# The last inverse transform of a convolution layer: transposes first, products by halves, output sent by halves

## The chip, the cores and the metric

The kernel runs on one core of a Trainium2 chip. The metric is the device time of one execution in microseconds. A time "of the profile" is on the clock of the one execution that was profiled, counted from its first instruction.

## The reference

The program has two layers on an image `x` of 2 x 128 channels x 64 x 64, that is 4096 tokens of 128 channels for each of two batches. Layer 0 is a group norm, a projection to queries, keys and values with rotary positions, attention with four heads, and a residual. Layer 1 is attention of the normalised tokens with themselves, and then a spectral unit: a causal convolution of the tokens with 16 filters, taken through Fourier transforms, mixed by matrices, plus a sum over three shifted copies of the tokens. Cut to what matters here:

```python
def _stu_conv(phi, u, n):
    Vf = jnp.fft.rfft(phi, n=n, axis=0)
    Uf_p = jnp.fft.rfft(u, n=n, axis=1)
    ...
    U_plus = jnp.fft.irfft(Vf[None, :, :, None] * Uf_p[:, :, None, :], n=n, axis=1)[:, :sl]
...
def _stu(u, sigma, phi, Mu, Mpp, Mpm):
    return _compute_spectral(u, sigma, phi, Mpp, Mpm) + _compute_ar_u(Mu, u)
...
t = t + _L1_attn_ref(_ln_t(t))
t = t + _L1_ffn_ref(_ln_t(t), ...)
x = _from_tokens(t, x)
```

`_compute_spectral` mixes the convolved signals with 2 x 16 matrices of 128 x 128. The result has the shape of `x`.

## The kernel before

Layer 0 runs first, then the attention of layer 1, then the spectral unit. The spectral unit writes a position as 32 j + i with j from 0 to 127 and i from 0 to 31, transforms along j with products on TensorE against a table of cosines and sines, convolves along i with the filters at each frequency, mixes with the matrices, and transforms back along j.

The last stage of the program goes through four passes, (batch, parity) = (0, 0), (0, 1), (1, 0), (1, 1), where the parity `ro` is that of i. In each pass there are eight chunks `ch` of frequencies and two signs `s`. For each, `chunk` loads filter tables (through SyncE's queue) and transformed tokens (through GpSimd's), `convolve` makes products `cv` and splits them into a high part `xh` (copied by ScalarE) and a low part `xl` (a subtraction on VectorE), and `mix` (L1208) multiplies both parts by the matrices and sums into `acc`, which at the end of a chunk is copied to a quarter of `oh`, 512 columns at a time (L1219). `mix` of a step is laid between the pieces of `convolve` of the next step, so TensorE always has products that wait for nothing. Tiles of `xh` come from a pool with two buffers of one tag; a new tile of the tag takes the place of the one before the last and waits for its readers.

`back` is the inverse transform of one pass. It takes the 16 blocks of i of its parity in four groups `p4` of four. For each group `turned` starts a load of `had` (256 KB: what the residual and the shifted copies add to the output) on SyncE's queue (L1238), transposes four 128 x 128 tiles for each of two parts c, cosine and sine (L1249), and copies them out of PSUM, part 0 on VectorE and part 1 on ScalarE, into `v` (L1250). `inverse` then makes eight products `bk` (L1258), two for each block, with a tile of `v` as the stationary operand and the 128 columns of `gw[:, c, :]` as the moving one, and adds `had` on VectorE into the output tile (L1260). That add writes every 32nd column, as the output is in the order of positions.

In three of the four passes `back` is a generator whose pieces are laid between those of the next pass. In the last pass (`end`) there is nothing to lie between. There the order is written out by hand: `turned(0)`, then for each group `turned` of the next one and `inverse` of this one; `v` takes buffers of the tag `xh`; the two parts of the transposes go to the two banks of one PSUM tile `pair` of the tag `cv`, which has three buffers; `had` is one buffer. At the very end the output of the batch goes to memory in four transfers of 512 KB, two from SyncE's queue and two from ScalarE's (L1275).

`ordered` keeps TensorE's instructions in the order of the program text. The waits between engines are worked out by the framework from which tile each instruction reads and writes. After the network, every engine reads a flag and branches over a second, general version of the network, which these inputs do not need.

## Time and profile before

| what | value |
|---|---|
| median of 3 runs | 2941.99 us (2936.91, 2941.99, 2942.27) |
| the profiled execution, its own time | 2936.34 us |
| span of the profile, first to last instruction | 2934.5 us |
| TensorE matmul busy | 2855.1 us, 97% of the span |
| VectorE / ScalarE / GpSimd busy | 58% / 65% / 23% |
| mean granted clock of TensorE | 0.992 |
| last mixing product to last instruction | 2903.9 to 2934.5 us |

PE stands for TensorE's products and PEld for its loads of the stationary operand, which overlap them; DVE is VectorE, ACT ScalarE, POOL GpSimd, SP SyncE, and a q behind a name means that engine's queue of instructions or transfers. A row of the timeline is: start in us, length in us, engine, line, operation, result <- operands, shapes, how many in a row, and in brackets the idle time before and what ended it. A row of the chain is: start, length, engine, what, how many. The output add stands in a row as `out<-bk,had`. A product in fp32 appears as two records. `first` and `m` are the PSUM tiles of layer 0's first projections and of the mixing.

### The profile page before, as it was taken

How to read it: one execution, taken by the hardware profiler on the slowest of the kernel's cores; microseconds unless marked ns; L12 is line 12 of the kernel's file. 1: busy time of each engine (PE TensorE's matmuls, PEld its weight loads, DVE VectorE, ACT ScalarE, POOL GpSimd, SP SyncE). 2: the span in 40 equal slices, each digit the busy share in tenths (PEclk: the TensorE clock that was granted, in tenths of full speed). 3: DMA queues.
4: the chain of work that ended last, by engine and by line, in shares of the span. 5: the costliest groups of instructions: out<-in, count | busy, mean ns of one | idle time of the engine just before them, and what ended most of it. 6: DMA issues, size and time to landing. Idle time of an engine off the chain costs nothing. (4 is left out here: it accounts for less than half of the span.)

```text
span 2934.5 us, 40078 instructions
## 1 busy us (share of the span) xinstructions
PE 2855.1 (97%) x13872; PEld 1817.6 (62%) x13872; DVE 1691.6 (58%) x2916; ACT 1916.2 (65%) x2507; POOL 660.9 (23%) x1328
## 2 busy tenths in 40 slices
PE   4999999999999999999999999999999999999997
PEld 2555555555455578787777885566666666666665
DVE  5264563255243289877766676555555555555553
ACT  4999999999999955565555664444444444444442
POOL 4031120022000010000102003434444444444440
PEclk9999999999999999999999999999999999999999
DMA  5021120021000024100011003333333334333331
GB/s 145 29 82 54 47 63 20 5 78 48 6 33 35 4 86 127 55 1 1 26 40 39 8 26 72 94 87 98 88 86 82 81 82 115 81 86 82 82 81 47
DMA packets 165777, 175.91 MB, mean 60 GB/s; under 512 B 45264, under 2 KB 109536, under 8 KB 165568
## 3 DMA queue, kind: packets, MB, share of 16 engines
q1 hardware_dynamic: 121760, 136.00, 16.7%
q0 software_dynamic: 40816, 34.04, 5.5%
q10 hardware_dynamic: 2992, 3.22, 0.3%
q8 instruction: 115, 1.88, 0.3%
q14 instruction: 94, 0.77, 0.1%
HBM read 130.68 MB, written 25.49 MB: 53 GB/s over the span
## 5 line engine op out<-in xcount | busy, mean ns | idle before, releaser
L433 ACT ACTIVATE e<-s 128x1536 f16<-128x1536 f32 (+1 forms) x704 | 936.7, 1428 | 35.8 <-PE s L190 30.9
L1186 DVE TENSOR_TENSOR xl<-cv,xh 128x1024 fp32r<-128x1024 f32 x512 | 603.3, 1220 | 436.6 <-ACT xh L1185 349.2
L1185 ACT CAST xh<-cv 128x1024 fp32r<-128x1024 f32 x512 | 494.6, 1018 | 523.1 <-PE cv L1176 511.7
L1151 POOL DMA_DIRECT2D tokens_in<-rows x1024 | 490.8, 487 | 680.6 <-PE cv L1176 577.7
L190 PE MATMUL s<-qs,ks 128*128 128x512 f16 x2048 | 557.4, 379 | 8.5 <-ACT e L433 3.4
L190 PE MATMUL acc<-e,v 128*97 128x512 f16 x2048 | 557.3, 379 | 3.4 <-DVE accs L389 0.2
L1208 PE MATMUL m<-xh,loT 128*128 128x512 f32 x1024 | 410.0, 400 | 0.0
L1208 PE MATMUL m<-xh,hiT 128*128 128x512 f32 x1024 | 403.5, 394 | 0.0
L190 PEld LDWEIGHTS <-v 128*97 128x97 bf16 x2048 | 254.6, 124 | 214.5 <-issue 12.3
L190 PEld LDWEIGHTS <-ks 128*128 128x128 f16 x2048 | 200.5, 99 | 227.6 <-issue 42.5
L910 ACT ACTIVATE ey<-y,nshift 128x512 f32<-128x512 f32 x288 | 195.9, 689 | 201.4 <-PE y L901 179.6
L1176 PE MATMUL cv<-tables_in,tokens_in 32*128 32x512 f32 x2048 | 299.4, 645 | 1.8 <-DVE xl L1186 1.8
L1208 PE MATMUL m<-xl,hiT 128*128 128x512 f32 x1024 | 292.3, 417 | 1.2 <-DVE xl L1186 0.5
L1208 PEld LDWEIGHTS m<-xl,hiT 128*128 128x128 f32 x1024 | 178.9, 189 | 175.8 <-issue 104.7
L1208 PEld LDWEIGHTS m<-xh,loT 128*128 128x128 f32 x1024 | 192.7, 188 | 90.8 <-issue 47.8
L1208 PEld LDWEIGHTS m<-xh,hiT 128*128 128x128 f32 x1024 | 192.6, 188 | 42.3
L920 DVE TENSOR_TENSOR eT<-eT,eT 128x512 fp32r<-128x512 f32 x224 | 147.5, 685 | 113.4 <-ACT eT L919 112.1
L927 PE MATMUL oacc<-ep,hi 128*128 128x512 f32 x576 | 210.4, 414 | 1.2 <-DVE ep L959 1.1
L389 DVE COPY accs<-acc 97x512 f32<-97x512 f32 x64 | 44.2, 691 | 275.2 <-PE acc L190 275.2
L959 DVE TENSOR_TENSOR ep<-ey,ep 128x512 fp32r<-128x512 f32 x288 | 191.5, 685 | 7.7 <-ACT ep L958 1.6
L919 ACT ACTIVATE eT<-eT 128x512 fp32r<-128x512 f32 x224 | 133.1, 605 | 55.6 <-PE eT L917 55.4
L927 PE MATMUL oacc<-eT,hi 128*128 128x512 f32 x448 | 154.1, 405 | 2.8 <-DVE oT L967 1.6
(192 smaller groups left out, 3045.2 us busy)
## 6 DMA issues: line engine op xcount, KB each, us to landing
tables_in<-tables SPq DMA_DIRECT2D x1024, 64.0 KB, 3.3
tab<-in_rot SPq DMA_DIRECT2D x32, 512.0 KB, 4.1
tokens_in<-rows POOLq DMA_DIRECT2D x1024, 16.0 KB, 3.2
qs<-term POOLq DMA_DIRECT2D x128, 64.0 KB, 2.2
rows<-uh SPq DMA_DIRECT2D x64, 128.0 KB, 1.9
ks<-term POOLq DMA_DIRECT2D x96, 64.0 KB, 1.9
accs<-back SPq DMA_DIRECT2D x32, 128.0 KB, 2.3
lows<-stage SPq DMA_DIRECT2D x16, 256.0 KB, 2.0
```

The costliest lines, as they stand in the source:

```text
L190: tc.keep_in_program_order(nc.tensor.matmul(*args, **kw))
L433: nc.scalar.activation(e[:, own, :], ps[:, own, :], AF.Exp, scale=SCORE_SCALE)
L910: nc.scalar.activation(e[:, 2 * h + q, :], ps[:, q, :], AF.Exp, bias=nshift, accum_out=den[:, t, i : i + 1])
L919: nc.scalar.activation(eT[0], pt, AF.Copy, accum_out=den[:, 4 * i + u, j : j + 1])
L920: nc.vector.tensor_tensor(eT[1], pt, eT[0], ALU.subtract)
L927: nc.tensor.matmul(acc, a[0][:, own], c, start=(start and t == 0 and n == 0), stop=(stop and t == len(es) - 1 and n == 2),)
L959: nc.vector.tensor_tensor(es[t][1], e[:, t, :], es[t][0], ALU.subtract)
L1151: nc.gpsimd.dma_start(ut[part, :, :], rows[b][ci, row : row + BP, w0 : w0 + WC // 2, :])
L1176: nc.tensor.matmul(pu[:, h, :], ut[grp, w % 2, :], tt[grp, w % 2, :], start=True, stop=True)
L1185: nc.scalar.copy(hi, pu.rearrange("d h (c k) -> d k h c", k=NK))
L1186: nc.vector.tensor_tensor(seconds[n % 2][:, :, w, 64 * g2 : 64 * g2 + 64].rearrange("d k (h c) -> d k h c", h=2), pu.rearrange("d h (c k) ...
L1208: nc.tensor.matmul(acc, m, x, start=(s == 0 and w == 0 and i == 0), stop=(s == 1 and w == WC - 1 and i == len(products) - 1),)
```

## The change

It touches only the last pass of `back`, the one with `end`. One tile `whole` of the tag `xh` holds all four groups: for each, four slots of 128 columns for `had` and eight for `v`. `turned` runs for all four groups first, so the four loads of `had`, the 32 transposes and the 8 copies come ahead of every product. Then the products go by halves `n` of the transformed length: for each half and each pair of groups a PSUM tile `pair` of two banks is taken, and each group's eight products write 4 x 64 columns into its bank, from the same stationary tiles and half the columns of `gw`. An add of half a group follows. After the four adds of a half, two of the four output transfers are started, one on SyncE's queue and one on ScalarE's.

```diff
-                had = p.tile([P, 4, P], F32, tag="had", name=f"had{u}", bufs=1)
+                if end:
+                    had, v = whole[:, p4, :4], whole[:, p4, 4:].rearrange("p (c q) x -> p c q x", c=2)
+                else:
+                    had = p.tile([P, 4, P], F32, tag="had", name=f"had{u}", bufs=1)
+                    v = p.tile([P, 2, 4, C], F32, tag="v", name=f"v{u}", bufs=1)
                 nc.sync.dma_start(had, baser[:, ro, 4 * p4 : 4 * p4 + 4, :])
-
-                v = (pf if end else p).tile(
-                    [P, 2, 4, C], F32, tag="xh" if end else "v", name=f"v{u}", bufs=2 if end else 1
-                )
...
-            ahead = list(turned(0)) if end else None
+            if end:
+                whole = pf.tile([P, BP // 4, 12, P], F32, tag="xh", name="whole", bufs=2)
+                parts = [list(turned(p4))[-1] for p4 in range(BP // 4)]
+                for n in range(2):
+                    js = bass.ts(n, P // 2)
+                    for p8 in range(BP // 8):
+                        pair = pc.tile([P, 2, 512], F32, tag="cv", name=f"bk{n}_{p8}", bufs=3)
+                        for h in range(2):
+                            p4 = 2 * p8 + h
+                            had, v = parts[p4]
+                            pt = pair[:, h, : 2 * P].rearrange("p (q j) -> p q j", q=4)
+                            for q in range(4):
+                                for c in range(2):
+                                    ordered(
+                                        nc.tensor.matmul(
+                                            pt[:, q, :], v[:, c, q, :], gw[:, c, js], start=(c == 0), stop=(c == 1)
+                                        )
+                                    )
+                            nc.vector.tensor_tensor(
+                                outr[:, ro, 4 * p4 : 4 * p4 + 4, js], pt, had[:, :, js], ALU.add
+                            )
+                    for i in range(2):
+                        cols = bass.ts(2 * n + i, L // 4)
+                        (nc.scalar if i % 2 else nc.sync).dma_start(io["out"][b][:, cols], outs[b][:, cols])
+                return
             for p4 in range(BP // 4):
-                if end:
-                    parts = ahead[-1]
-                    ahead = list(turned(p4 + 1)) if p4 + 1 < BP // 4 else None
-                else:
-                    for parts in turned(p4):
-                        yield
+                for parts in turned(p4):
+                    yield
                 inverse(p4, *parts)
                 yield
```

## The prediction

> **What bounds the kernel now.** I read the page first, then the chain of work that ended last, then the timeline of the last 35 us, which is all that the diff can touch: apart from renamed tiles, every engine's instruction order before the last block's transposes is the same in both programs.

> ```profile
> span 2934.5 us, 40078 instructions
> PE 2855.1 (97%) x13872; PEld 1817.6 (62%) x13872; DVE 1691.6 (58%) x2916; ACT 1916.2 (65%) x2507; POOL 660.9 (23%) x1328
> ```

> TensorE holds the kernel for 97% of the span, and the change leaves that alone. What it edits is the tail after TensorE's last mixing product, where no engine is full. The chain, in order of time (start, length, what):

> ```profile
> 2892.44 11.42 PE m L1208 x48
> ...
> 2903.89 0.59 ACT oh L1219
> ...
> 2906.02 1.17 PE vt L1249 x8
> 2907.19 0.02 issue
> 2907.22 0.70 DVE v L1250
> ...
> 2916.93 1.80 PE bk L1258 x16
> 2918.73 0.02 issue
> 2918.76 1.03 DVE out L1260
> 2919.79 0.02 issue
> 2919.81 2.92 DMA had<-base
> ...
> 2922.82 1.02 DVE out L1260
> ```

> The reader is to see a ladder: transposes, copy, products (1.80 each block), add, and in the last block a load of `had` that ends after the products. The timeline adds both ends of it:

> ```profile
> 2919.83 2.05 PE L1258 MATMUL bk<-gw,v 128*128 128x128 f32 x16 [1.12 <-DVE out L1260]
> 2922.82 1.02 DVE L1260 TENSOR_TENSOR out<-bk,had 128x512 f32<-128x512 f32 x1 [3.04 <-DMA had<-base]
> 2923.87 0.83 SPq L1275 DMA_DIRECT2D out<-out  x2
> ```

> The last products end at 2921.88, their add begins at 2922.82: 0.94 us for `had`. The four output transfers (2.1 MB) go out together at 2923.87; the stretches of 1 us after it move 123, 397, 389, 418, 373, 369, 61 GB/s, so the data flow from about 2924.7 to 2930.15 at some 390 GB/s. The span ends at 2934.5, 10.66 us after the last add.

> What the change turns on is the price of a product with 64 moving columns in place of 128. Layer 0 has products of just that form, and the timeline of weight loads shows both:

> ```profile
> 30.83 0.86 PEld L190 LDWEIGHTS first<-wv,xn 128*128 128x128 f32 x7 [0.24 <-issue]
> 2908.40 1.87 PEld L1258 LDWEIGHTS bk<-gw,v 128*128 128x128 f32 x16
> ```

> The first has 64 moving columns, the second 128. A load lasts 0.19, so the steps are (0.86 - 0.19) / 6 = 0.112 and (1.87 - 0.19) / 15 = 0.112 us. Half the columns, the same step: the weight load sets it.

> [...]

> **The change part by part.** Times are on the trace's clock; the oh copy ends at 2904.48 in both.

> *Transposes first.* Before, a block's second four transposes wait for the vector copy of the first four, because both write one tile of two banks; the changed program keeps that wait. The pace without products between is the one from 2906.02 to 2907.96: 1.94 us (1.16 of transposes, 0.70 copy, gaps). So second halves begin at 2906.02, 2907.96, 2909.90, 2911.84. Products follow 0.55 after a second half (2907.96 to 2908.51): first product 2912.39. The ScalarE copies (0.59 each) end within 1.5 us of their transposes, ahead of the products that need them.

> *Products by halves.* Eight groups of eight products, each two records: 16 x 0.112 = 1.80 us, as much as a whole block now. TensorE's work here goes from 4 x 1.80 = 7.2 to 14.4 us: +7.2. The stationary operand is the transposed block, so each is loaded twice.

> *A new wait.* Two groups share one tile of two banks. The changed program's order shows the second group waiting for the vector engine's count that the add of the first raises: the same rule that stalls the transposes. Behind that product stand all later ones, so it is paid four times. Each costs what a non-waiting group hides: products end, add, restart. From the trace: 1.99 us from a running group's start to its add (2908.51 to 2910.50), 2.08 when the group starts after a wait (2919.83 to 2921.88, plus 0.03), 0.05 from an add's end to the products.

> *The add of half a block*, 256 elements. Not in the trace. [...] Lower bound the contiguous 0.42, upper the whole block's 1.02. I take 0.59, since the excess over the contiguous add should go with elements.

> So: add 1 begins 2912.39 + 1.99 = 2914.38. A pair takes 0.59 + 0.05 + 2.08 to its second add, and 1.80 more to the next pair's first: 4.52. Add 4 ends at 2914.38 + 4.52 + 2.72 + 0.59 = 2922.21; add 8 at 2914.38 + 3 x 4.52 + 2.72 + 0.59 = 2931.25. Before it was 2923.84: +7.41.

> *Halves of the output.* The first two transfers go at about 2922.2 and by the rates above are in by about 2926.4; 5 us of products cover them. After add 8 only 1.05 MB are left in place of 2.1: 1.05 / 0.39 = 2.7 us less. The end: 2931.25 + 10.66 - 2.7 = 2939.2. If nothing were gained by sending early, +2.7. On SyncE and ScalarE only the second half's transfers stand behind the first's, and those are ready later anyway; ScalarE's copies are all ahead of them. GpSimd's queue issues nothing in this stretch.

> *Loads of `had`.* Now four into one tile, which takes the place of the `xh` of the step before the last, read by TensorE until 2891.92. SyncE is done with tables by then. Four issues of 0.38 and 3.0 to land put them in by 2897, under mixing products, 17 us before the first add. The 0.94 us wait goes (it is inside the sum); without that cover 1.05 MB at the 230 GB/s of the present loads would cost some 4.5 us.

> Sum: +7.4 - 2.7 = **+4.7 us on the span of 2934.5, so 2939.2**. The profiled execution took 2936.34; the median of three is 2941.99 (2936.91 to 2942.27), so the profile sits at the low end. I put the difference on the median: 2941.99 + 4.7 = **2946.7 us**, 0.16% slower, inside the 0.2% that a measurement of this kernel can tell from no change.

> **The rivals.**
> 1. *Half an add costs nearly a whole one* (the slower side). If the excess of L1260 sits in each instruction rather than each element, four exposed adds cost up to 1.02 for 0.59: +1.7, so +6.4, 2948.4, 0.22%. For it: a single size in the trace. Against it: the contiguous rows scale. It passes 0.2% (5.9 us) once the add takes 0.89.
> 2. *No wait within a pair.* Then eight groups run on at 1.80: the last add begins at 2912.39 + 7 x 1.80 + 1.99 = 2926.98, 3.7 earlier: +1.0, 2943.0. Against it: the transposes of this very tile stall so in the trace.
> 3. *Half the columns, half the time.* Groups of 0.9: each pair saves 1.8, 7.2 in all: -2.5, 2939.5. Against it: the row of layer 0.
> 4. *The change doesn't do what it says*: the first half's output is held until the second's goes. Then -2.7 is lost: +7.4, 2949.4. Against it: its wait names only the first four adds.

> **How the numbers follow.** My account 0.64, rival 1 0.12, rival 2 0.08, rival 3 0.05, rival 4 0.04, other 0.07. Faster by over 0.2% comes from almost none of them: rival 3 with a low median. But +4.7 stands only 1.2 us below the bound, and three runs spread over 5.4 us, so of my own account I give a third to slower; with two thirds of rival 1, rival 4 and half of the rest that makes slower 0.37, faster 0.05, same 0.58. The range: rivals 2 and 3 with a median at the low end reach 2940; rivals 1 and 4 with one at the high end reach 2951. My account's own is 2942 to 2949.

> **What would show it.** Eight groups of `bk` with 64 columns, weight loads of 1.87 us per 16; four waits of TensorE for the adds, 0.7 us each (0.03 + 0.59 + 0.05; the one before, 1.12, had a whole add in it); half adds of 0.59; no wait for `had`; the first output transfers some 9 us ahead of the second; from the last add to the end about 8.0 in place of 10.66. I am wrong if the 64-column loads step below 0.1, if the half add is near 1.0, if the tail after the last add stays above 9.5, or if the median moves by something before 2903.

## The result and the profile after

The changed kernel took 2957.45 us (median of 4 runs, 2953.83 to 2960.28) against 2940.3 us for the kernel before (2936.91 to 2942.27): the ratio is 1.0065, with a 95% interval of 1.0053 to 1.0077. The forecast was 2946.7 and a range up to 2951: it is slower, as forecast, but the loss is 17 us where 4.7 had been worked out.

The profiled execution has a span of 2952.0 us. Up to the first transpose of the last pass nothing moved: it starts at 2904.72 after 2904.53. The whole difference lies behind it. The chain of work that ended last, in order of time (start, length, engine, what, how many):

```profile
2904.72 0.73 PE vt L1249 x4
...
2912.05 0.71 PE vt L1249 x4
2912.77 3.32 PE bk L1278 x16
2916.09 0.02 issue
2916.11 0.59 DVE out L1282
2916.71 0.04 issue
2916.76 7.10 PE bk L1278 x32
...
2940.06 3.69 PE bk L1278 x16
2943.74 0.02 issue
2943.77 0.59 DVE out L1282
```

The ladder has the rungs that the prediction named, in its order: transposes at 1.94 us a group, products, an add of 0.59, four waits of the products inside pairs. One rung is wrong. Sixteen records of half-width products take 3.3 to 3.7 us, not 1.80. The timeline of the same stretch shows the loads and the output:

```profile
2928.86 15.88 SPq L1287 DMA_DIRECT2D out<-out  x2
...
2932.29 6.90 PEld L1278 LDWEIGHTS bk<-gw,whole 128*128 128x128 f32 x32 [0.87 <-DVE out L1282]
2932.29 7.09 PE L1278 MATMUL bk<-gw,whole 128*128 128x64 f32 x32 [0.68 <-DVE out L1282]
2936.00 0.60 DVE L1282 TENSOR_TENSOR out<-bk,whole 128x256 f32<-128x256 f32 x1 [3.77 <-PE bk L1278]
```

A load now lasts 0.33, so the step is (6.90 - 0.33) / 31 = 0.212 us (the starts of single loads lie 0.213 apart), where it was 0.112. The busy time of each engine by stretches tells why (columns: stretch, its length, busy us and instructions of each engine, then TensorE's granted clock as a share of full speed, the share of the transfer engines, GB/s). Before, for the whole of the last pass:

```profile
2903.90:2923.90 20.00, 12.30 (x96) 11.16 (x96) 6.50 (x8) 2.92 (x5) 0.00 (x0) 1.00 0.14 41
```

After:

```profile
2911.00:2912.00 1.00, 0.27 (x3) 0.08 (x1) 0.69 (x1) 0.44 (x1) 0.00 (x0) 1.00 0.06 16
2912.00:2913.00 1.00, 0.95 (x7) 0.95 (x8) 0.00 (x0) 0.20 (x1) 0.00 (x0) 0.82 0.00 0
2913.00:2914.00 1.00, 1.00 (x7) 1.00 (x6) 0.00 (x0) 0.39 (x1) 0.00 (x0) 0.50 0.00 0
...
2940.00:2944.00 4.00, 3.67 (x16) 3.49 (x16) 0.23 (x2) 0.00 (x0) 0.00 (x0) 0.50 0.02 4
```

The granted clock falls from 1.0 to 0.5 at 2912.6, as the last transposes end, and stays there through all 31 us of products. In the kernel before, it was 1.0 until 2926.9, five microseconds after the last product. Note how little the page shows of this: TensorE counts as busy all the time, and the clock's row has a single 7 in its last place.

The size fits: 128 loads at 0.21 in place of 0.112 are 128 x 0.10 = 12.8 us, and 4.7 + 12.8 = 17.5, which is the difference of the spans.

What brings the clock down, and what keeps it down? At 0.112 us a record, 64 columns fill only part of the step. How much follows from rows of layer 0 in the kernel before, plain fp32 products of 512 columns, the first two at a clock of 1.0 and the third at 0.5, which it had there from 39.3 to 46.1 us:

```profile
29.54 0.59 PE L190 MATMUL first<-xn,wqk 128*128 128x512 f32 x1
29.97 1.02 PE L190 MATMUL first<-xn,partner 128*128 128x512 f32 x2
43.69 1.91 PE L190 MATMUL first<-xn,partner 128*128 128x512 f32 x2
```

One record takes 0.59 us and two take 1.02, so they step by 0.43: 0.84 ns a column, an estimate of the time for which a column streams. So 128 columns stream for 0.107 us, 96% of a step; 64 for 0.054, 48%. At half clock the same records step by 0.85 (their loads start at 42.84, 43.69 and 44.55), 1.67 ns a column; the loads of narrow products step by 0.213 in place of 0.112, and 64 columns are 50% of 0.213. A stretch is called dense or thin below by the share of it in which columns stream. The theory that I set out with was that the run of transposes drops the clock; the rivals were that this form of product is slow by itself, that the gaps between products do it, and that it is the density of the streamed columns.

### The profile page after: what moved, and what is told of

Read it like the earlier page. It is cut to its first block, busy times and chain, and to the rows that moved or that the text cites. A ratio compares the mean times of both kernels' runs of the same rounds, so it can differ in the third digit from the quotient of the medians.

```text
span 2952.0 us, 40206 instructions
## 1 busy us (share of the span) xinstructions
PE 2875.5 (97%) x13936; PEld 1837.5 (62%) x13936; DVE 1691.8 (57%) x2920; ACT 1915.6 (65%) x2507; POOL 658.3 (22%) x1328
## 5 line engine op out<-in xcount | busy, mean ns | idle before, releaser
L190 PE MATMUL s<-qs,ks 128*128 128x512 f16 x2048 | 557.5, 379 | 8.5 <-ACT e L433 3.4
L190 PE MATMUL acc<-e,v 128*97 128x512 f16 x2048 | 557.3, 379 | 3.4 <-DVE accs L389 0.2
L1208 PE MATMUL m<-xh,loT 128*128 128x512 f32 x1024 | 409.6, 400 | 0.0
L1208 PE MATMUL m<-xh,hiT 128*128 128x512 f32 x1024 | 403.0, 394 | 0.0
L190 PEld LDWEIGHTS <-v 128*97 128x97 bf16 x2048 | 254.6, 124 | 214.3 <-issue 12.4
L190 PEld LDWEIGHTS <-ks 128*128 128x128 f16 x2048 | 200.6, 99 | 227.6 <-issue 42.5
L1208 PE MATMUL m<-xl,hiT 128*128 128x512 f32 x1024 | 292.3, 418 | 1.2 <-DVE xl L1186 0.5
L1208 PEld LDWEIGHTS m<-xl,hiT 128*128 128x128 f32 x1024 | 178.8, 189 | 175.8 <-issue 104.7
L1208 PEld LDWEIGHTS m<-xh,loT 128*128 128x128 f32 x1024 | 192.6, 188 | 90.7 <-issue 47.8
L1208 PEld LDWEIGHTS m<-xh,hiT 128*128 128x128 f32 x1024 | 192.4, 188 | 42.2
```

Source lines behind the costliest of these rows:

```text
L190: tc.keep_in_program_order(nc.tensor.matmul(*args, **kw))
L1208: nc.tensor.matmul(acc, m, x, start=(s == 0 and w == 0 and i == 0), stop=(s == 1 and w == WC - 1 and i == len(products) - 1),)
```

## The experiments

From one execution to the next, the stretch ahead of the last pass is some us longer or shorter, so beside each median I give the tail: from the first transpose of the last pass to the end of the span. It was 30.0 us before (2904.53 to 2934.5) and 47.3 after; the prediction's is 34.7. The experiments were measured in three series, each with the kernel before beside them: it took 2937.8 us in the first two (18 and 29 runs) and 2937.3 in the last (23). Ratios are to these.

### Filler products in the gaps of the transposes

```diff
+                    if end and c == 0:
+                        fill = one_bank(f"fill{u}")
+                        for k in range(3):
+                            ordered(nc.tensor.matmul(fill, mxr[:, k, 0, :], xl[:, bass.ts(k, 512)], start=True, stop=True))
                     (nc.scalar.copy if c else nc.vector.tensor_copy)(v[:, c, :, :], pt)
```

> The changed kernel with three more products of 512 columns in the gap behind each group's first four transposes (their result is used by nothing). Theory, clock: TensorE's granted clock falls to 0.5 during the run of transposes because those alone do not hold it; with the fillers it stays at 1.0, the weight loads of the 64-column products step by 0.112 us, and the span shrinks by 12 to 14 us against the changed kernel, to about 2939. Rival, form: these 64-column products take 0.21 us a record by themselves: the step stays 0.21 and the span at about 2952. Third: the fillers hold the clock at first, and it falls later, within the thin products; then between the two.

Measured: 2949.49 us (six runs, 2944.81 to 2953.84), ratio 1.0037 (1.0024 to 1.0050); tail 45.2, in the longest of the six runs; three of them, at 2944.8 to 2948.0, had a mean clock of 0.991 in place of 0.988. The fillers held the clock through the transposes, and the form is not slow: the first sixteen loads take 1.87 us, as in the kernel before. Then, in the second group of products, at 2918.3, it falls. The timeline of loads:

```profile
2914.67 1.87 PEld L1282 LDWEIGHTS bk<-gw,whole 128*128 128x128 f32 x16
2917.36 6.08 PEld L1282 LDWEIGHTS bk<-gw,whole 128*128 128x128 f32 x32 [0.81 <-DVE out L1286]
```

and the stretches:

```profile
2907.00:2914.70 7.70, 7.36 (x44) 5.45 (x45) 2.77 (x4) 1.76 (x3) 0.00 (x0) 1.00 0.01 2
2914.70:2918.00 3.30, 2.62 (x25) 2.48 (x23) 0.58 (x1) 0.59 (x1) 0.00 (x0) 1.00 0.00 0
2919.00:2944.00 25.00, 22.47 (x102) 21.72 (x101) 3.99 (x7) 0.00 (x0) 0.00 (x0) 0.50 0.11 43
```

The third expectation, then: the form is out as a cause, and the transposes are not needed for it: the clock was 1.0 past their end, and fell behind half-width products with a gap.

### All transposes first, but whole products

```diff
-                for n in range(2):
-                    js = bass.ts(n, P // 2)
...
-                                            pt[:, q, :], v[:, c, q, :], gw[:, c, js], start=(c == 0), stop=(c == 1)
+                                        pt[:, q, :], v[:, c, q, :], gw[:, c, :], start=(c == 0), stop=(c == 1)
```

Adds and output are whole too, four transfers at the end.

> All transposes first, but whole products of 128 columns, whole adds and the output in four transfers at the end. Clock: the clock falls about 8 us after the oh copy as in the changed kernel; if it stays low, the weight loads step by 0.21 to 0.22 us, the last add ends near 2930 and the span is about 2941, 6 to 7 us over the kernel before. If products of 128 columns are dense enough to bring it back, 3 us. Rival, form: with 128 columns nothing is slow, the loads step by 0.112, the span is within 1 us of the kernel before.

Measured: 2938.09 us (12 runs), ratio 1.0005 (0.9996 to 1.0014); tail 29.5. In the profile the clock is 1.0 through the same run of transposes, as well as through the products:

```profile
2905.00:2912.90 7.90, 4.64 (x32) 3.88 (x33) 2.77 (x4) 1.82 (x4) 0.00 (x0) 1.00 0.01 2
2912.90:2924.00 11.10, 7.94 (x67) 7.37 (x65) 3.99 (x4) 0.58 (x1) 0.00 (x0) 1.00 0.00 1
```

So putting the transposes first costs nothing by itself, most of the time. Ten runs lie between 2935.9 and 2940.4 with a mean clock of 0.991 to 0.993; two lie at 2945.0 and 2945.1 with 0.989. Those 7 us are what was expected if the clock falls in the transposes; no trace shows these two. In the traces of the kernels before and after, the stretches between two changes of the clock are multiples of 3.413 us long (before: 6.83 us at 0.5 from 39.26, then 27.30 at 1.0, 3.41 at 0.5, 959.14 at 1.0). If such a grid decides, whether a thin stretch of 8 us is caught would depend on how it lies to the grid: sometimes. My first theory said always.

### Halves, with the transposes between the products

```diff
-                parts = [list(turned(p4))[-1] for p4 in range(BP // 4)]
+                parts = [list(turned(0))[-1]]
                 for n in range(2):
+                    for p4 in range(BP // 4):
+                        if n == 0 and p4 + 1 < BP // 4:
+                            parts.append(list(turned(p4 + 1))[-1])
+                        if n == 0:
+                            pair, h = one_bank(f"bk{n}_{p4}").rearrange("p (h x) -> p h x", h=1), 0
...
```

The edit changes a second thing: in the first half each group's products have a tile of one bank to themselves and form no pairs; the last of these groups still waits 0.68 us for the add ahead of it.

> Products by halves and output by halves, but each group's transposes lie between the products of the first half, as in the kernel before. Clock: [...]the clock holds at 1.0, loads step by 0.112 us, the span is about 2939, 4 to 5 us over the kernel before and 13 us under the changed one. Rival, form: step 0.21 and a span of 2950 or more. Third: the thin products alone (second half) do not hold the clock, and it falls in the second half: 2943 to 2946.

Measured: 2948.1 us (5 runs, 2946.75 to 2952.79), ratio 1.0038 (1.0024 to 1.0053); tail 40.2. The clock holds through the interleaved part and falls at 2920.4, at the end of the first half:

```profile
2917.00:2920.30 3.30, 2.62 (x24) 2.48 (x23) 0.59 (x1) 0.00 (x0) 0.00 (x0) 1.00 0.00 0
2920.50:2937.00 16.50, 14.44 (x66) 13.87 (x65) 2.96 (x5) 0.00 (x0) 0.00 (x0) 0.50 0.16 65
```

This again was the third case, and the profile's span of 2944.9 lies in its 2943 to 2946. Putting the transposes between the products does not save the halves either.

### Plain products in place of the transposes

```diff
-                        ordered(nc.tensor.transpose(pt[:, q, :], ohr[:, c, BP - 1 - 4 * p4 - q, :], ident))
+                        own = ohr[:, c, BP - 1 - 4 * p4 - q, :]
+                        if end:
+                            ordered(nc.tensor.matmul(pt[:, q, :], own, ident, start=True, stop=True))
...
```

> The changed kernel with its 32 transposes made as plain fp32 products with the identity, in the same places. If it is the transpose mode that does not count for the clock, the clock stays at 1.0, the products step by 0.112 us, and the span is about 2942 (the transposing products have two records each, 3 us more). If it is the low share of work of TensorE in that stretch, whatever the kind, the clock falls at the same place and the span is about 2955.

Measured: 2965.85 us (4 runs), ratio 1.0094 (1.0077 to 1.0111); tail 58.1. It can't answer its question, for it changed a second thing: a plain product loads the strided tile of `oh` in steps of 0.220 us at full clock (eight loads in 1.83 us, the last of them 0.29), where transposes of the same tile step by 0.111 (eight loads in 0.97 us, the last of them 0.19). So these products were thin as well. But what the clock does tells something. It falls, comes back for one stretch, and falls again:

```profile
2905.60:2909.90 4.30, 3.52 (x15) 3.33 (x15) 0.69 (x1) 0.00 (x0) 0.00 (x0) 1.00 0.00 0
2910.00:2916.70 6.70, 5.92 (x26) 5.55 (x25) 0.69 (x1) 1.17 (x2) 0.00 (x0) 0.50 0.01 2
2916.80:2920.10 3.30, 2.52 (x12) 2.41 (x12) 0.69 (x1) 0.35 (x1) 0.00 (x0) 1.00 0.00 0
2920.20:2924.00 3.80, 3.02 (x13) 2.72 (x13) 0.69 (x1) 0.13 (x1) 0.00 (x0) 0.50 0.00 0
```

At full clock 128 columns stream for 0.107 of 0.220 us, 49%; at half clock the step hardly changes (0.217: 16 loads in 3.58 us) and the columns would take 0.214 of it, nearly all. The same instructions are thin at full clock and dense at half, and the clock went with that share and not with the instructions. Whether transposes count less than products, the traces together answer below.

### All columns streamed in each half

```diff
-                                            pt[:, q, :], v[:, c, q, :], gw[:, c, js], start=(c == 0), stop=(c == 1)
+                                            pt[:, q, :], v[:, c, q, :], gw[:, c, :], start=(c == 0), stop=(c == 1)
```

Each half computes all columns, and its adds (not in the cut) read 64 of them.

> The changed kernel, but each half's products stream all 128 columns of the table; the adds still take 64 of them. Loads, order, waits, adds and transfers stay; only the columns streamed by a product double. Theory, density: it is products of 64 columns behind loads of 128 that leave the array too idle to hold the clock; with 128 the clock stays at 1.0 in nearly every run, loads step by 0.112 us, and the span is about 2939 (the prediction's sum), 13 us under the changed kernel. Rival, gaps: the waits between transposes and between halves bring the clock down; nothing changes here, the step stays near 0.21 to 0.22 and the span at 2952 or more.

Measured: 2943.92 us (18 runs, 2940.02 to 2949.95), ratio 1.0019 (1.0012 to 1.0026), 6.1 us over the kernel before beside it where the change was 17.2 over: doubling the columns of every product makes the kernel some 11 us faster. In the profile (tail 40.3) the clock had already fallen in the transposes, at 2907.9; the products brought it back at 2921.6, with the same waits of 0.68 us between them:

```profile
2913.39 3.54 PEld L1278 LDWEIGHTS bk<-gw,whole 128*128 128x128 f32 x16
2917.90 5.39 PEld L1278 LDWEIGHTS bk<-gw,whole 128*128 128x128 f32 x32 [0.97 <-DVE out L1282]
2924.17 3.65 PEld L1278 LDWEIGHTS bk<-gw,whole 128*128 128x128 f32 x32 [0.87 <-DVE out L1282]
```

The third row has 32 loads in 3.65 us, the step of 0.112. The five fastest runs (2940.0 to 2941.2, mean clock 0.993) are 2 to 3 us over the kernel before, somewhat under the prediction's 4.7. The span of this profile, 2944.4, isn't the 2939 expected, because of the 13.7 us at half clock. The gaps as sole cause are out: they are all still there, and the clock came back.

### A tile of its own for each half group

```diff
-                        pair = pc.tile([P, 2, 512], F32, tag="cv", name=f"bk{n}_{p8}", bufs=3)
                         for h in range(2):
                             p4 = 2 * p8 + h
+                            pair = pc.tile([P, 2, 512], F32, tag="cv", name=f"bk{n}_{p4}", bufs=3)
...
```

> The changed kernel with a PSUM tile of its own for each half group: the four waits of 0.68 us of TensorE for adds go, the 64 thin products run on without a gap. Gaps: without them the clock holds or comes back, the step is 0.112, span near 2936. Density: a run of 64-column products without a gap does not hold the clock either; loads step by 0.21 for most of it, and only the waits' price goes, four times 0.7 us: span 2948 to 2950.

Measured: 2949.96 us (8 runs), ratio 1.0033 (1.0020 to 1.0046), but in two groups: three runs at 2937.8 to 2942.4 (mean clock 0.991 to 0.993) and five at 2949.7 to 2952.3 (0.987 to 0.988). Each expectation had one of the groups. The profile is of the first, tail 31.3, and has what the gaps' side expected: 128 loads of half-width products in one go at full speed, with the clock at 1.0 to their end.

```profile
2917.07 14.38 PEld L1278 LDWEIGHTS bk<-gw,whole 128*128 128x128 f32 x128
```

```profile
2917.00:2931.50 14.50, 14.50 (x132) 14.45 (x130) 4.19 (x7) 0.58 (x1) 0.00 (x0) 1.00 0.19 73
```

A stream of 64 columns without gaps held a clock that was high for these 14.5 us; the density side had been wrong there. The second group has the time of a clock that fell in the transposes and never came back; no trace shows it, so that part is inferred. The profile is also the cleanest trial of the prediction's other terms: 34.7 less the four waits, each of which cost 0.59 + 0.05 + 2.08 - 1.80 = 0.92 us, is 31.0; the tail is 31.3.

### 96 columns, then 32

```diff
-                    js = bass.ts(n, P // 2)
+                    js = slice(96 * n, 96 + 32 * n)
...
```

Three of the four output transfers go behind the first part (not in the cut).

> The changed kernel cut unevenly: the first part has 96 columns and three of the four output transfers, the second 32 and the last. Density: with 96 columns a product streams for about 70% of its step against 48% with 64, so the clock should hold longer or throughout the first part (if it does not fall in the transposes already)[...]; span 2940 to 2948. Gaps: as the changed kernel, 2952, give or take the transfers.

Measured: 2950.49 us (5 runs, 2942.57 to 2951.29), ratio 1.0038 (1.0025 to 1.0051); tail 40.5. The profile's span is 2948.3, at the end of the 2940 to 2948 that the density side expected. The clock fell at the end of the transposes (2915.4), came back after 3.4 us, most of them with 96-column products, and fell for good (2929.0) after the first 16 records of 32 columns:

```profile
2915.40:2918.70 3.30, 3.30 (x18) 3.30 (x17) 0.00 (x0) 0.58 (x1) 0.00 (x0) 0.50 0.00 0
2918.80:2929.00 10.20, 7.96 (x68) 7.52 (x66) 3.62 (x5) 0.00 (x0) 0.00 (x0) 1.00 0.05 18
2929.10:2940.00 10.90, 10.44 (x48) 10.30 (x48) 0.74 (x2) 0.00 (x0) 0.00 (x0) 0.50 0.32 126
```

### Own tiles for the transposes too

```diff
-                if end:
-                    pair = pc.tile([P, 2, 512], F32, tag="cv", name=f"vt{u}", bufs=3)
...
-                    pt = pair[:, c, :] if end else one_bank(f"vt{u}_{c}")
+                    if end:
+                        pt = pc.tile([P, 2, 512], F32, tag="cv", name=f"vt{u}_{c}", bufs=3)[:, 0, :]
+                    else:
+                        pt = one_bank(f"vt{u}_{c}")
```

This goes on top of the tile for each half group; the halves and the early output are those of the change.

> The changed kernel (64-column halves, output by halves) with a PSUM tile of its own for each quad of transposes and for each half group, so that neither waits. Theory as it stands: the run of transposes shrinks from 8 to about 4.2 us, too short to bring the clock down, and a stream of 64-column products without gaps holds a clock that is high; step 0.112, last add near 2921.6, span about 2929 to 2930, 4 us over the version with whole products and 5 us under the kernel before. If 64-column products bring the clock down by themselves even without gaps, loads step by 0.21 from some point on and the span is 2935 to 2942.

Measured: 2934.02 us (20 runs, 2931.36 to 2941.12), ratio 0.9988 (0.9982 to 0.9995): the change with its waits taken out is a little faster than the kernel before. Tail 27.7, clock 1.0 to the end of the products. The transposes take 3.9 us:

```profile
2911.50:2915.40 3.90, 3.87 (x31) 3.76 (x32) 2.31 (x4) 1.76 (x3) 0.00 (x0) 1.00 0.00 0
2915.40:2930.00 14.60, 14.53 (x131) 14.39 (x129) 4.69 (x9) 0.59 (x1) 0.00 (x0) 1.00 0.19 74
```

The profile's span of 2939.2 is not the 2929 to 2930 that was expected: this execution reached its last pass 7 us late, and the median is that of other executions.

### Own tiles and whole products

The transposes' tiles as in the last one; whole products as in the second, each group in a tile of its own; the last add in two halves, so that two transfers start between them.

```diff
+                        pair = pc.tile([P, 2, 512], F32, tag="cv", name=f"bk{p4}", bufs=3)
...
+                        for n in range(2) if p4 == BP // 4 - 1 else ():
+                            js = bass.ts(n, P // 2)
+                            nc.vector.tensor_tensor(
+                                outr[:, ro, 4 * p4 : 4 * p4 + 4, js], pt[:, :, js], had[:, :, js], ALU.add
+                            )
```

> A version meant to beat both: transposes first, each quad of them in a PSUM tile of its own, whole products of 128 columns in a tile of their own for each group, the last add in two halves with the first two output transfers behind the first of them. Density: the clock holds; no waits of 0.78 us between quads and of 1.1 us within a pair; last products end near 2917, the output goes 0.6 us later, span about 2928, 6 to 7 us (0.2%) under the kernel before. Rival, gaps or the run of transposes: if the clock falls in the transposes, loads step by 0.21, and it ends near 2935.

Measured: 2928.29 us (6 runs, 2927.22 to 2930.53), ratio **0.9968 (0.9956 to 0.9980)**: faster than both kernels. Tail 22.7 (2902.35 to 2925.1), of which the whole products are one row without a gap:

```profile
2902.34 3.97 PEld L1250 LDWEIGHTS vt<-ident,oh 128*128 128x128 f32 x32 [1.10 <-ACT oh L1219]
2906.23 7.23 PEld L1277 LDWEIGHTS bk<-gw,whole 128*128 128x128 f32 x64
```

The span is 3 us under the 2928 expected, 2.2 of them ahead of the last pass. Against the version before it, the halves cost 27.7 - 22.7 = 5.0 us: 7.2 of loads, less what sending half of the output early gives back.

### The clock against the width of the products

The fastest version with eleven runs of 128 products each behind its own, without gaps, whose results nothing uses.

```diff
+                for m, width in enumerate((128, 96, 80, 64, 48, 32, 48, 64, 80, 96, 128)):
+                    for r in range(16):
+                        scan = pc.tile([P, 2, 512], F32, tag="cv", name=f"scan{m}_{r}", bufs=3)
```

> The version with whole products, and after its products eleven more runs of 128 products each, with no gaps and results that nothing uses: 128, 96, 80, 64, 48, 32, 48, 64, 80, 96, 128 columns. At full clock each run takes about 28.7 us, whatever its width, if the load sets the step; at half clock about 55. Density with a lag: going down, the clock holds at 64 (two profiles show it did for 14 us at most) and falls at 48 or 32 (36% and 24% of a step streaming at full clock); going up it stays low at 48 and 64 (38% and 50% at half clock) and comes back at 80 or 96. If the clock were set by gaps alone it would stay at 1.0 throughout.

Measured, from one execution, stretches of the eleven runs in order, of these products alone (length, products, loads, granted clock, share of the transfer engines, GB/s):

```profile
2970.70:2999.20 28.50, 28.50 (x258) 28.50 (x256) 1.00 0.00 1
2999.30:3027.80 28.50, 28.50 (x258) 28.50 (x257) 1.00 0.01 1
3027.90:3077.80 49.90, 49.90 (x257) 49.90 (x256) 0.55 0.00 1
...
3187.30:3241.70 54.40, 54.40 (x257) 54.40 (x257) 0.50 0.00 1
3241.90:3296.30 54.40, 54.40 (x257) 54.40 (x257) 0.50 0.00 1
3296.50:3327.80 31.30, 31.30 (x257) 31.30 (x256) 0.90 0.00 1
3327.90:3356.40 28.50, 28.50 (x258) 28.50 (x256) 1.00 0.01 2
```

These are 80, 64 and 48 columns on the way down, 64, 80, 96 and 128 on the way up. Width didn't change a run's time as long as the clock held: 28.5 us for 128 as for 64. Without a gap the clock held at 64 and fell within 48 (1.00 to 3032.0, 0.50 from 3033.0); it stayed low at 64 and 80, and came back within 96 (0.50 to 3302.0, 1.00 from 3303.0). In estimated shares of streaming, by the 0.84 and 1.67 ns a column above: at full clock 48% held and 36% did not; at half clock 63% did not bring it back and 75% did. The two marks are apart: the same 64 columns ran at full speed on the way down (28.5 us) and at half on the way up (54.4), by what was there before them.

The traces together show more. In those of the kernels before and after, the changes of the clock lie on one grid of 3.413 us: the shortest stretch between two changes is one step of it (73.39 to 76.81 before, 72.75 to 76.16 after), the longest 331 steps (1797.12 to 2926.93 before). In the experiments the distances fit it as far as the rows place them: 6.8 and 3.4 us with plain products, 13.7 with all columns, 3.4 and 10.2 with 96 columns and 32. Lay the grid through the last changes in seven traces (before, after, fillers, interleaved, plain products, all columns, 96 and 32), and count the time for which columns stream in each stretch of the last pass up to its last product, at 0.84 ns a column at full clock and twice that at half, a transpose as one record of 128 columns (for the mixing products 0.445 ns, as their records of 512 columns step by 0.228 us). This is an estimate of the streamed share, from the rows of the timelines:

| behind the stretch | estimated share of streaming in it |
|---|---|
| 1.0, then 0.5 | 39% after; 37 or 38% fillers; 37% interleaved; 33 and 37% plain products; 37% all columns; 37 and 34% 96 and 32 |
| 1.0, then 1.0 | lowest: 41% before; 42% interleaved; 45% 96 and 32; 50% after |
| 0.5, then 1.0 | 73% 96 and 32; 92% plain products; 100% all columns |
| 0.5, then 0.5 | highest: 75% and then 68% all columns; 62% plain products; 51% fillers |

At full clock no stretch is on the wrong side, though 39 and 41% are closer than the estimate is sure. At half clock it can't tell the sides apart between 73 and 75%. The transposes must count in full for this: a stretch of 16 of them and nothing else, 50%, held the clock in the changed kernel (2905.81 to 2909.22).

So in these traces it is the streamed share of a stretch that goes with the clock of the next, and gaps, narrow products and transposes all lower it. In the changed kernel the stretch from 2909.22 to 2912.64 has 12 transposes and the first narrow product, 39%, and the clock fell behind it. With whole products it held through the same transposes; how the grid lay to them there was not shown. With the fillers and in the interleaved version, the stretch ahead of the fall has nothing but narrow products and one wait: some 37% in both.

## Why the prediction was wrong

The step that failed is "Half the columns, the same step: the weight load sets it", carried from full clock into a stretch that loses it. At full clock 0.112 us is right, and the fillers' first sixteen loads and both versions with a tile for each half group have it. The prediction took the clock of 1.0 along as if it were a property of the chip, and did not ask what the change does to it. Its two rows came from other surroundings: eight records between products of 512 columns, and whole products in stretches of the kernel before that stream 45% or more by the count above. The record of the kernel before held the other price too: where layer 0 runs at half clock, at 45.4 us, single records of that very row, 64 columns wide, start 0.213 us apart. Here the narrow products, with a wait in each pair, follow a run of transposes. The term of 14.4 us measured 27.3 (128 x 0.213); 12.9 more, where the tail was 12.6 longer than the sum had it. The waits, the add, the output and the loads of `had` came as forecast, so the sign rests on costs that are there at full clock, but most of the loss does not come from them.

Loads slowed with the clock as products did: a load of 128 columns stepped by 0.213 us where the granted clock was 0.5, and by 0.112 where it was 1.0.

Point by point:

- *Transposes first*: 1.94 us a group, first product 7.88 us behind the first transpose; predicted 7.86. Right. That they may cost the clock was missed; it fell in them in three of the profiles with transposes in this order and at this pace (after, all columns, 96 and 32) and not in two (whole products, own tile for each half group).
- *A new wait*: four, 0.68 us each for 0.7 predicted. Right, and rival 2 is out.
- *The add of half a block*: 0.584 to 0.601 us for 0.59. Right; rival 1 is out. The trace of before leads to it by itself: its contiguous adds take 0.424 us for 256 elements (L363) and 0.689 for 512 (L1017), L1260 takes 1.018, and 0.424 with half of the excess of 0.329 is 0.59, an estimate. At 384 and 128 elements (96 and 32 columns) it took 0.80 to 0.83 and 0.37, on the same line.
- *Halves of the output*: from the last add's end (2944.36) to the span's, 7.7 us for 8.0. Right. The first half left 15 us ahead of the second (2928.86 and 2944.39), 9 having been predicted, so rival 4 is out.
- *Loads of had*: issued at 2892.15, waited for by nobody. Right.
- *Rival 3*, half the columns in half the time: wrong by a factor of nearly four.
- *Sign and range*: slower, as the sum said, but "same" had been given the larger chance. The range was built from rivals that all had TensorE at full clock; the one that came true was not among them, and the list of what would show me wrong looked for loads faster than 0.112, not slower.

What carried the change's idea, sending half of the output early, works: from the last add to the end it took 7.7 us in place of 10.6, and 8.7 in the version with own tiles for all. Its price, every stationary tile loaded twice, is 7.2 at full clock and 20 at half.

## What to carry to other kernels

A price per product held here only while the granted clock did: 0.112 us at 1.0, 0.213 at 0.5. Before splitting products along the moving side, work out in which share of a step the columns stream, take the waits in, and ask what the clock does there. Here it fell behind 3.4 us with an estimated 33 to 39% and stayed up behind 41% or more; once at half, without gaps, 63% did not bring it back and 75% did. In a tail, look first for waits that come from two uses of one tile. Own PSUM tiles for each quad and group, together with a last add in two parts, brought the version with whole products from 0.05% over the kernel before to 0.32% under it; with the gaps closed, the clock was 1.0 through its transposes and products (2902.3 to 2914.0).
